# Pinning TensorE to "turn two groups, then multiply two groups" in a 30-step recurrence, with the first copy out of PSUM cut in two

## The chip, the cores and the metric

The kernel runs on one core of one Trainium2 chip. The metric is the device time of one execution in microseconds (us); lower is better. Engines are named as the profile names them: PE is TensorE's matmuls and PEld its weight loads, DVE is VectorE, ACT is ScalarE, POOL is GpSimd, and SP is the engine that issues most DMAs.

## The reference: what is computed

The input x has 3327 rows of 256 numbers. Two layers follow, each a graph attention and then a feed-forward part: in layer 0 a mixture of 16 experts, in layer 1 a recurrence over 30 steps. The change touches the recurrence alone. Cut to what matters, it is

```
def step(h, _):
    h = h + 0.01 * jnp.tanh(h)
    h = h * jax.nn.sigmoid(h)
    h = _layernorm(h, ln_w, ln_b)
    h = jnp.einsum('bsc,dc->bsd', h, W) + b
    return (h, None)
x, _ = jax.lax.scan(step, x, None, length=30)
```

Rows don't depend on each other. Each row goes through 30 steps in order, and its result is added to what came into the recurrence. Everything is fp32.

## The kernel before

The 3327 rows lie in SBUF as 26 tiles of 128 rows, `x` of 128 x 26 x 256. The recurrence works on groups of G = 4 tiles: six groups of four and a last one of two, seven in all (`groups`). Two nested loops, 30 steps outside and seven groups inside, emit this for each group (lines 992 to 1029):

- ScalarE makes `th = tanh(hs / S)` of the group (L998). The state is kept scaled by S = 100, so that POOL's sum `th + hs` (L1000) is the scaled `h + 0.01 tanh(h)`. ScalarE's Silu of it gives `z` (L1001).
- VectorE takes the statistics of each tile (`bn_stats`, L1006), and TensorE turns the tile by two 128 x 128 transposes into `pt` in PSUM (L1008): eight transposes for a group of four tiles. `pt` takes two PSUM banks, two tiles in each.
- `inv_norm` (L981 to L990) aggregates the statistics on VectorE (`v`, L986) and raises the variance to the power -1/2 on POOL (`rr`, L988 and L989).
- ScalarE copies the whole of `pt` to `zT` in SBUF, in one instruction (L1010).
- TensorE multiplies: for each tile two matmuls over the halves of the 256 features into `po` in PSUM (L1014). The weight that is loaded is a 128 x 128 piece of `zT`, and the matrix `wc` streams past it. An fp32 matmul stands in the profile as two records and a transpose as one; so a group of four has 8 transposes and 16 product records.
- VectorE scales by `rr` and adds the bias `bb`, tile by tile, back into `x` (L1019). The mean of the layer norm was folded into `wc` before.
- In the last step alone, a DMA brings what came into the recurrence (`old`, L1025), VectorE adds it (L1026) and DMAs write the output (L76).

The order of the work is not written by hand. The program is traced in Python, and a scheduler of the framework then orders each engine's instructions by its own estimates of time, taking the one traced first where several are ready. That order is fixed in the program: on the chip each engine works through its own list and waits on semaphores. Buffers limit how far it can run ahead: `th`, `z`, `zT`, `pt` and `po` have two buffers each, the small tiles of statistics four. In the step shown further down, TensorE's list has the runs that the timeline shows: 16 transposes, 32 product records, and at the end of a step runs of 10, 8 and 10.

Other stages matter only for comparison. In the projection of layer 1, `turned` (L141 to L149) turns two tiles by four transposes (L147), ScalarE copies one bank (L148), and `products` (L158 to L165) multiplies the two tiles turned before them (L162).

The lines about the copy and the two loops:

```
                for j in range(n):
                    nc.vector.bn_stats(stats[:, j, :], z[:, j, :])
                    for k in range(KD):
                        nc.tensor.transpose(pt[:, j, k, :], z[:, j, k * P : (k + 1) * P], ident)
                rr = inv_norm(stats, n)
                nc.scalar.copy(zT[:, :n, :, :], pt[:, :n, :, :])
```

Of the kernel before, what the change touches and what calls it, by code (L numbers as in the profile page):

```python
# [11 lines left out]
F32 = mybir.dt.float32  # L12
# [3 lines left out]
AF = mybir.ActivationFunctionType  # L16
ALU = mybir.AluOpType
# [3 lines left out]
P = 128  # L21
ALPHA = 0.2
EPS = 1e-5
N_STEPS = 30
S = 100.0
G = 4
# [4 lines left out]
def gat_moe_gat_recurrent_ffn(ctx: ExitStack, tc: tile.TileContext, a: dict, out: bass.AP):  # L31
    nc = tc.nc
    N, D = a["x"].shape
    KD = D // P
# [9 lines left out]
    groups = [range(t, min(t + G, NT)) for t in range(0, NT, G)]  # L44
# [9 lines left out]
    def spread(n):  # L54

        cut = n - n % 16
        return [r for r in ((0, cut), (cut, n)) if r[0] < r[1]]
# [6 lines left out]
    small = ctx.enter_context(tc.tile_pool(name="small", bufs=4))  # L64
# [3 lines left out]
    x = state.tile([P, NT, D], F32, name="x")  # L68
# [4 lines left out]
    def move_pairs(dram, tile, c0, c1, into_dram):  # L73

        def move(dst, src):
            nc.sync.dma_start(*((dst, src) if into_dram else (src, dst)))  # L76

        full = min(c1, PAIRS - 1)
        if full > c0:
            move(  # L80
                dram[c0 * 2 * P : full * 2 * P, :].rearrange("(t p b) d -> p t (b d)", p=P, b=2),
                tile[:, : 2 * (full - c0), :].rearrange("p (t b) d -> p t (b d)", b=2),
            )
        if c1 == PAIRS:
            base, last = (PAIRS - 1) * 2 * P, 2 * (PAIRS - 1 - c0)
            for r0, r1 in spread(REST // 2):
                move(
                    dram[base + 2 * r0 : base + 2 * r1, :].rearrange("(p b) d -> p (b d)", b=2),
                    tile[r0:r1, last : last + 2, :].rearrange("p b d -> p (b d)"),
                )  # L90
            if REST % 2:
                move(dram[base + REST - 1 : base + REST, :], tile[REST // 2 : REST // 2 + 1, last, :])
# [265 lines left out]
    with ExitStack() as moe:  # L358
# [5 lines left out]
        part = route_p.tile([P, 1], F32, name="part")  # L364
# [16 lines left out]
        ps_o = moe.enter_context(tc.tile_pool(name="ps0o", bufs=2, space=PSUM))  # L381
# [5 lines left out]
        with ExitStack() as pre:  # L387
# [83 lines left out]
            for k in range(2):  # L471
                numbers(pair[:, :, k, 0], [[P, NT]], k * NP, 1)
            nc.gpsimd.affine_select(
                out=before, in_=ones, pattern=[[1, P]], compare_op=ALU.is_gt, fill=0.0, base=0, channel_multiplier=-1
# [144 lines left out]
        two = rec.tile([P, 2, SLOTS], F32, name="prod")  # L619
# [252 lines left out]
        bb = rec.tile([P, D], F32, name="bb")  # L872
# [17 lines left out]
    kept = dram.tile([NP, D], F32, name="kept")  # L890
    steps = ctx.enter_context(tc.tile_pool(name="steps", bufs=2))
    with ExitStack() as st:
# [8 lines left out]
        ps_o = st.enter_context(tc.tile_pool(name="ps2o", bufs=2, space=PSUM))  # L901
# [74 lines left out]
    with ExitStack() as st:  # L976
        ps_t = st.enter_context(tc.tile_pool(name="ps3t", bufs=2, space=PSUM))
        ps_o = st.enter_context(tc.tile_pool(name="ps3o", bufs=2, space=PSUM))
        last_p = st.enter_context(tc.tile_pool(name="last", bufs=2))

        def inv_norm(stats, n):  # L981


            v = small.tile([P, G, 2], F32, name="v")
            for j in range(n):
                nc.vector.bn_aggr(v[:, j, :], stats[:, j, :])  # L986
            r = small.tile([P, G], F32, name="rr")
            nc.gpsimd.tensor_scalar(r[:, :n], v[:, :n, 1], EPS, None, op0=ALU.add)  # L988
            nc.gpsimd.tensor_tensor(r[:, :n], r[:, :n], neg_half[:, :n], ALU.pow)  # L989
            return r  # L990

        for step in range(N_STEPS):
            for ts in groups:
                n = len(ts)
                hs = x[:, ts[0] : ts[0] + n, :]
                th = steps.tile([P, G, D], F32, name="th")
                z = steps.tile([P, G, D], F32, name="z")
                nc.scalar.activation(th[:, :n, :], hs, AF.Tanh, scale=1.0 / S)  # L998

                nc.gpsimd.tensor_tensor(th[:, :n, :], th[:, :n, :], hs, ALU.add)  # L1000
                nc.scalar.activation(z[:, :n, :], th[:, :n, :], AF.Silu, scale=1.0 / S)  # L1001
                stats = small.tile([P, G, 6], F32, name="stats")
                pt = ps_t.tile([P, G, KD, P], F32, name="pt")
                zT = steps.tile([P, G, KD, P], F32, name="zT")
                for j in range(n):
                    nc.vector.bn_stats(stats[:, j, :], z[:, j, :])  # L1006
                    for k in range(KD):
                        nc.tensor.transpose(pt[:, j, k, :], z[:, j, k * P : (k + 1) * P], ident)  # L1008
                rr = inv_norm(stats, n)
                nc.scalar.copy(zT[:, :n, :, :], pt[:, :n, :, :])  # L1010
                po = ps_o.tile([P, G, D], F32, name="po")
                for j in range(n):
                    for k in range(KD):
                        nc.tensor.matmul(  # L1014
                            po[:, j, :], lhsT=zT[:, j, k, :], rhs=wc[:, k, :],
                            start=(k == 0), stop=(k == KD - 1),
                        )
                for j in range(n):
                    nc.vector.scalar_tensor_tensor(  # L1019
                        x[:, ts[0] + j, :], po[:, j, :], rr[:, j : j + 1], bb, op0=ALU.mult, op1=ALU.add  # L1020
                    )
                if step == N_STEPS - 1:
                    here = slice(ts[0] * P, (ts[-1] + 1) * P)
                    old = last_p.tile([P, G, D], F32, name="old")
                    nc.sync.dma_start(old[:, :n, :], kept[here, :].rearrange("(t p) d -> p t d", p=P))  # L1025
                    nc.vector.scalar_tensor_tensor(  # L1026
                        hs, hs, 1.0 / S, old[:, :n, :], op0=ALU.mult, op1=ALU.add
                    )
                    move_pairs(out, hs, ts[0] // 2, (ts[-1] + 1) // 2, True)


# [47 lines left out]
```

The softmax here doesn't subtract the row's maximum and nothing guards it: scores larger than these inputs give would overflow.

## Time and profile before

| what | us |
|---|---|
| three runs, without the profiler | 1998.33, 2000.29, 2000.75; median 2000.29 |
| the profiled execution, its own time | 2004.62 |
| its span, first to last instruction | 2002.9 |
| first transpose of the recurrence to the end of the span | 1098.5 to 2002.9 |
| ten steps of the recurrence, 1400 to 1699: PE, DVE, ACT, POOL busy | 291.95, 218.46, 188.99, 236.43 of 299 |
| TensorE's granted clock in that stretch | 1.00 of full speed |

The profile is of one execution. In a timeline each line is a run of equal instructions on one engine: its start in us from the start of the span, its length, the engine, the line of the kernel, output and inputs, shapes, count, and in brackets how long the engine had idled before and which engine's instruction ended that. In the list of groups, a line has the count, then the busy time in us and the mean length of one in ns, then the idle time ahead of them and its enders. Records of matmuls overlap each other, since their ends are modelled; the time between two starts is the measure of their rate.

### The profile page before, as it was taken

The page shows a single profiled execution, that of the slowest core. Times are in us where ns is not written, and L with a number is a line of the kernel's source. Part 1 is how long each engine was busy: PE and PEld are TensorE (multiplying, and loading weights), DVE is VectorE, ACT ScalarE, POOL GpSimd, SP SyncE. Part 2 cuts the span into 40 slices and gives each one's busy share as a digit, 9 for nine tenths or more (in the row PEclk, how much of TensorE's full clock was granted, in tenths as well). Part 3 has the DMA queues.
Part 4 walks back from the last instruction along what each step waited for, and adds up shares of the span by engine and source line. Part 5 has one row for each costly group of instructions (what it writes and reads, how often), then busy time and mean ns, then how long its engine had stood idle before and what let it go on. Part 6 is the DMA issues. An engine that isn't in the chain of part 4 may idle for free.

```text
span 2002.9 us, 33524 instructions
## 1 busy us (share of the span) xinstructions
PE 1930.9 (96%) x12032; PEld 1750.0 (87%) x12032; DVE 1299.7 (65%) x3827; ACT 1095.5 (55%) x1419; POOL 938.4 (47%) x864
## 2 busy tenths in 40 slices
PE   7999999999999997999999999999999999999998
PEld 6999999989999986888888888888888888888887
DVE  6887888722222226567576777777777777777777
ACT  2967766621111115566555666666666666666664
POOL 3020212443333321001000787787787787787785
PEclk9999999999999998999999999999999999999999
DMA  8978141189999854000001000000000000000003
GB/s 165 119 100 119 10 76 50 39 291 324 351 330 308 297 195 137 9 8 17 9 17 35 1 1 1 1 1 1 1 1 1 1 1 1 1 1 1 1 1 116
DMA packets 139754, 157.08 MB, mean 78 GB/s; under 512 B 52027, under 2 KB 99364, under 8 KB 139586
## 3 DMA queue, kind: packets, MB, share of 16 engines
q1 hardware_dynamic: 123466, 122.05, 19.8%
q0 software_dynamic: 11440, 28.09, 8.1%
q10 hardware_dynamic: 4680, 4.76, 0.7%
q8 instruction: 98, 1.61, 0.3%
q14 instruction: 70, 0.57, 0.1%
HBM read 164.58 MB, written 29.78 MB: 97 GB/s over the span
## 4 chain that ended last, share of the span: by engine, by line
PE 68%; issue 9%; ACT 5%; POOL 5%; DVE 4%; DMA 3%; SPq 0%; another core or an unknown queue 0%; POOLq 0%; DVEq 0%; ACTq 0%
PE po L1014 35%; PE acc L262 23%; PE pt L1008 5%; ACT zT L1010 5%; DVE pT L257 2%; POOL given L831 2%; POOL rb L730 2%; DMA given<-wh,to 2%; PE bank L786 2%; PE acc L827 1%; PE bank L499 1%; PE bank L221 0%; DVE x L913 0%; PE acc L162 0%; POOL rstd L120 0%
## 5 line engine op out<-in xcount | busy, mean ns | idle before, releaser
L1014 PE MATMUL po<-wc,zT 128*128 128x256 f32 x3120 | 705.5, 383 | 21.7 <-ACT zT L1010 21.1
L1014 PEld LDWEIGHTS po<-wc,zT 128*128 128x128 f32 x3120 | 583.1, 190 | 124.1 <-ACT zT L1010 49.7
L252 ACT ACTIVATE e<-rb,minus,full 128x384 f32<-128x384 f32 (+3 forms) x494 | 400.2, 824 | 180.9 <-DVE pT L257 162.7
L1000 POOL TENSOR_TENSOR th<-th,x 128x1024 f32<-128x1024 f32 (+1 forms) x210 | 460.8, 2213 | 64.3 <-ACT th L998 62.7
L257 DVE SCALAR_TENSOR_TENSOR pT<-e,part,adjT 128x384 f32<-128x384 f32 (+3 forms) x494 | 381.1, 776 | 138.1 <-PE acc L262 117.5
L1019 DVE SCALAR_TENSOR_TENSOR x<-po,rr,bb 128x256 f32<-128x256 f32 x780 | 324.9, 478 | 118.3 <-PE po L1014 113.8
L1010 ACT COPY zT<-pt 128x1024 f32<-128x1024 f32 (+1 forms) x210 | 199.0, 947 | 334.0 <-PE pt L1008 334.0
L1006 DVE BATCH_NORM_STATS2 stats<-z 128x6 f32<-128x256 f32 x780 | 283.7, 415 | 117.6 <-ACT z L1001 117.6
L262 PE MATMUL acc<-wh,pT 128*128 128x129 f32 x2704 | 310.4, 276 | 1.8 <-DVE pT L257 1.8
L262 PEld LDWEIGHTS acc<-wh,pT 128*128 128x128 f32 x2704 | 305.2, 192 | 2.5 <-DVE pT L257 2.4
L262 PE MATMUL acc<-s_wh,pT 128*128 128x257 f32 x1352 | 295.3, 380 | 0.8 <-DVE pT L257 0.7
L262 PEld LDWEIGHTS acc<-s_wh,pT 128*128 128x128 f32 x1352 | 255.9, 190 | 37.7 <-DVE pT L257 1.8
L120 POOL TENSOR_TENSOR rstd<-ve,neg_half 128x4 f32<-128x4 f32 (+3 forms) x28 | 30.4, 1086 | 415.7 <-DVE ve L118 332.1
L989 POOL TENSOR_TENSOR rr<-rr,neg_half 128x4 f32<-128x4 f32 (+1 forms) x210 | 208.0, 990 | 17.4
L1001 ACT ACTIVATE z<-th 128x1024 f32<-128x1024 f32 (+1 forms) x210 | 210.6, 1003 | 0.6 <-POOL th L1000 0.5
L998 ACT ACTIVATE th<-x 128x1024 f32<-128x1024 f32 (+1 forms) x210 | 199.3, 995 | 1.9 <-DVE x L127 0.9
L1008 PE MATMUL pt<-ident,z 128*128 128x128 f32 x1560 | 191.6, 274 | 2.5 <-DVE high L944 2.5
L1008 PEld LDWEIGHTS pt<-ident,z 128*128 128x128 f32 x1560 | 179.5, 142 | 14.9 <-issue 2.9
L786 PEld LDWEIGHTS bank<-hT,wh 128*128 128x128 f32 x1280 | 150.7, 194 | 9.2 <-issue 4.8
L786 PE MATMUL bank<-hT,wh 128*128 128x128 f32 x1280 | 151.8, 277 | 6.6 <-issue 2.2
L820 DVE TENSOR_TENSOR pT<-e,bank 128x512 f32<-128x512 f32 x61 | 41.9, 687 | 176.9 <-PE bank L786 124.2
L816 ACT ACTIVATE e<-bank 128x512 f32<-128x512 f32 x61 | 36.4, 597 | 194.1 <-PE bank L786 90.3
(189 smaller groups left out, 1346.4 us busy)
## 6 DMA issues: line engine op xcount, KB each, us to landing
wh<-in_w_dram SPq DMA_DIRECT2D x120, 512.0 KB
first_set<-in_w_dram SPq DMA_DIRECT2D x63, 512.0 KB
in_bytes<-in_adj_dram POOLq DMA_DIRECT2D x3, 2496.0 KB
x<-in_x_dram SPq DMA_DIRECT2D x6, 512.0 KB
kept<-x SPq DMA_DIRECT2D x8, 384.0 KB
old<-kept SPq DMA_DIRECT2D x6, 512.0 KB
out_dram<-x SPq DMA_DIRECT2D x6, 512.0 KB
table_x<-row ACTq DMA_DIRECT2D x3, 768.0 KB
```

The source lines that it names most:

```text
L252: nc.scalar.activation(e[:, : n * P], rb[:, : n * P], AF.Relu, scale=sc.full[:, j, h : h + 1], bias=sc.minus[:, j, h : h + 1],)
L257: masked = nc.vector.scalar_tensor_tensor(pT[:, : n * P], e[:, : n * P], sc.part[:, j, h : h + 1], adjT[:, j // 2, ts[0] * P : (ts[-1] + 1 ...
L262: nc.tensor.matmul(po[c], lhsT=pT[:, c * P : (c + 1) * P], rhs=wh[:, j, h, :], start=(j == 0 and c % per_bank == 0), stop=(j == NT - 1), s ...
L786: nc.tensor.matmul(p[:, f, :], lhsT=w[:, k, f * P : (f + 1) * P], rhs=hT[:, k, :], start=(k == 0), stop=(k == KD - 1),)
L989: nc.gpsimd.tensor_tensor(r[:, :n], r[:, :n], neg_half[:, :n], ALU.pow)
L1000: nc.gpsimd.tensor_tensor(th[:, :n, :], th[:, :n, :], hs, ALU.add)
L1001: nc.scalar.activation(z[:, :n, :], th[:, :n, :], AF.Silu, scale=1.0 / S)
L1006: nc.vector.bn_stats(stats[:, j, :], z[:, j, :])
L1008: nc.tensor.transpose(pt[:, j, k, :], z[:, j, k * P : (k + 1) * P], ident)
L1010: nc.scalar.copy(zT[:, :n, :, :], pt[:, :n, :, :])
L1014: nc.tensor.matmul(po[:, j, :], lhsT=zT[:, j, k, :], rhs=wc[:, k, :], start=(k == 0), stop=(k == KD - 1),)
L1019: nc.vector.scalar_tensor_tensor(x[:, ts[0] + j, :], po[:, j, :], rr[:, j : j + 1], bb, op0=ALU.mult, op1=ALU.add)
```

## The change

The body of the loop is cut into two functions. `turn_group` holds everything up to the transposes. `next_state` holds the rest: the power, the copy, the products and the update. The 210 parts (30 steps of seven groups, in one sequence across the ends of steps) are taken two at a time: two turns, then two next states. Each transpose and each matmul of the recurrence is passed to `tc.keep_in_program_order`, a method of the framework that puts an instruction behind the one traced just before it on the same engine; it orders the list and adds no wait. So TensorE's list is the traced order: turn A, turn B, products of A, products of B, then the next two. The other engines' lists are still the scheduler's. The copy of the first group of each two is made in pieces of two tiles (`pieces` = 2: two instructions for a group of four tiles, one for the group of two); the second group's copy stays whole.

```diff
-        for step in range(N_STEPS):
-            for ts in groups:
...
+        def turn_group(ts):
...
+            pt = ps_t.tile([P, G, KD, P], F32, name="pt")
+            for j in range(n):
+                nc.vector.bn_stats(stats[:, j, :], z[:, j, :])
+                for k in range(KD):
+                    tc.keep_in_program_order(
                         nc.tensor.transpose(pt[:, j, k, :], z[:, j, k * P : (k + 1) * P], ident)
-                rr = inv_norm(stats, n)
-                nc.scalar.copy(zT[:, :n, :, :], pt[:, :n, :, :])
-                po = ps_o.tile([P, G, D], F32, name="po")
-                for j in range(n):
-                    for k in range(KD):
+                    )
+            return pt, stats
+
+        def next_state(step, ts, pt, stats, pieces):
+            n = len(ts)
+            hs = x[:, ts[0] : ts[0] + n, :]
+            rr = inv_norm(stats, n)
+            zT = steps.tile([P, G, KD, P], F32, name="zT")
+            for c in range(0, n, G // pieces):
+                some = slice(c, min(c + G // pieces, n))
+                nc.scalar.copy(zT[:, some, :, :], pt[:, some, :, :])
+            po = ps_o.tile([P, G, D], F32, name="po")
+            for j in range(n):
+                for k in range(KD):
+                    tc.keep_in_program_order(
                         nc.tensor.matmul(
                             po[:, j, :], lhsT=zT[:, j, k, :], rhs=wc[:, k, :],
                             start=(k == 0), stop=(k == KD - 1),
                         )
...
+        parts = [(step, ts) for step in range(N_STEPS) for ts in groups]
+        for i in range(0, len(parts), 2):
+            two = [part + turn_group(part[1]) for part in parts[i : i + 2]]
+            for part, pieces in zip(two, (2, 1)):
+                next_state(*part, pieces)
```

More of the change, by code (lines that the diff above doesn't have):

```diff
@@ L990, in inv_norm @@
             return r
-        for step in range(N_STEPS):
-            for ts in groups:
[L994 to L1004, printed above, removed]
-                for j in range(n):
-                    nc.vector.bn_stats(stats[:, j, :], z[:, j, :])
-                    for k in range(KD):
-                        nc.tensor.transpose(pt[:, j, k, :], z[:, j, k * P : (k + 1) * P], ident)
-                rr = inv_norm(stats, n)
-                nc.scalar.copy(zT[:, :n, :, :], pt[:, :n, :, :])
-                po = ps_o.tile([P, G, D], F32, name="po")
-                for j in range(n):
-                    for k in range(KD):
@@ new lines, in turn_group @@
+        def turn_group(ts):
+            n = len(ts)
+            hs = x[:, ts[0] : ts[0] + n, :]
+            th = steps.tile([P, G, D], F32, name="th")
+            z = steps.tile([P, G, D], F32, name="z")
+            nc.scalar.activation(th[:, :n, :], hs, AF.Tanh, scale=1.0 / S)
+            nc.gpsimd.tensor_tensor(th[:, :n, :], th[:, :n, :], hs, ALU.add)
+            nc.scalar.activation(z[:, :n, :], th[:, :n, :], AF.Silu, scale=1.0 / S)
+            stats = small.tile([P, G, 6], F32, name="stats")
+            pt = ps_t.tile([P, G, KD, P], F32, name="pt")
[3 more added lines that the diff above has]
+                    tc.keep_in_program_order(
+                        nc.tensor.transpose(pt[:, j, k, :], z[:, j, k * P : (k + 1) * P], ident)
+                    )
+            return pt, stats
@@ new lines, in next_state @@
+        def next_state(step, ts, pt, stats, pieces):
+            n = len(ts)
+            hs = x[:, ts[0] : ts[0] + n, :]
+            rr = inv_norm(stats, n)
[7 more added lines that the diff above has]
+                    tc.keep_in_program_order(
@@ L1017, in gat_moe_gat_recurrent_ffn @@
                         )
-                for j in range(n):
-                    nc.vector.scalar_tensor_tensor(
-                        x[:, ts[0] + j, :], po[:, j, :], rr[:, j : j + 1], bb, op0=ALU.mult, op1=ALU.add
-                    )
[L1022 to L1029, printed above, removed]
+                    )
+            for j in range(n):
+                nc.vector.scalar_tensor_tensor(
+                    x[:, ts[0] + j, :], po[:, j, :], rr[:, j : j + 1], bb, op0=ALU.mult, op1=ALU.add
+                )
+            if step == N_STEPS - 1:
+                here = slice(ts[0] * P, (ts[-1] + 1) * P)
+                old = last_p.tile([P, G, D], F32, name="old")
+                nc.sync.dma_start(old[:, :n, :], kept[here, :].rearrange("(t p) d -> p t d", p=P))
+                nc.vector.scalar_tensor_tensor(hs, hs, 1.0 / S, old[:, :n, :], op0=ALU.mult, op1=ALU.add)
+                move_pairs(out, hs, ts[0] // 2, (ts[-1] + 1) // 2, True)
+        parts = [(step, ts) for step in range(N_STEPS) for ts in groups]
[3 more added lines that the diff above has]
+                next_state(*part, pieces)
 _OUT = ((3327, 256), "float32")
```

## The prediction

> **What bounds the kernel now.** I read four views in this order. First the page: TensorE's busy share, and the costliest groups.
>
> ```profile
> PE 1930.9 (96%) x12032; PEld 1750.0 (87%) x12032; DVE 1299.7 (65%) x3827; ACT 1095.5 (55%) x1419; POOL 938.4 (47%) x864
> ...
> L1014 PE MATMUL po<-wc,zT 128*128 128x256 f32 x3120 | 705.5, 383 | 21.7 <-ACT zT L1010 21.1
> L1014 PEld LDWEIGHTS po<-wc,zT 128*128 128x128 f32 x3120 | 583.1, 190 | 124.1 <-ACT zT L1010 49.7
> L1010 ACT COPY zT<-pt 128x1024 f32<-128x1024 f32 (+1 forms) x210 | 199.0, 947 | 334.0 <-PE pt L1008 334.0
> ```
>
> See that TensorE and ScalarE wait for each other over one edge, the copy zT. Records of matmuls overlap (383 ns each, started 216 ns apart), so "busy" and the 21.7 us of idle time hide what a wait costs. Second, therefore, TensorE's timeline, read by start times: one step of the recurrence, 1426.15 back to 1396.25, lasts 29.90 us.
>
> ```profile
> 1407.85 1.91 PE L1008 MATMUL pt<-ident,z 128*128 128x128 f32 x16
> 1409.99 7.17 PE L1014 MATMUL po<-wc,zT 128*128 128x256 f32 x32 [0.23 <-ACT zT L1010]
> 1417.00 1.91 PE L1008 MATMUL pt<-ident,z 128*128 128x128 f32 x16
> 1419.14 7.17 PE L1014 MATMUL po<-wc,zT 128*128 128x256 f32 x32 [0.23 <-ACT zT L1010]
> 1426.15 1.26 PE L1008 MATMUL pt<-ident,z 128*128 128x128 f32 x10
> 1427.43 1.99 PE L1014 MATMUL po<-wc,zT 128*128 128x256 f32 x8
> 1429.26 1.25 PE L1008 MATMUL pt<-ident,z 128*128 128x128 f32 x10
> 1430.74 7.17 PE L1014 MATMUL po<-wc,zT 128*128 128x256 f32 x32 [0.23 <-ACT zT L1010]
> ```
>
> TensorE already turns two groups and then forms two products in most places. The rate inside a run: transposes (1.91 - 0.273)/15 = 0.109 us; product records, from the second (1410.31) to the thirty-first (1416.57) of one run, 6.26/29 = 0.216 us. A pair at these rates is 16 x 0.109 + 32 x 0.2157 = 8.65 us; it takes 1417.00 - 1407.85 = 9.15. So **0.50 us is lost per pair**: 0.39 ahead of the first product (2.14 against 1.74) and 0.11 behind it (7.01 against 6.90). At the end of a step (10, 8, 10) the 8-record run loses 0.19 + 0.10 = 0.29. A step loses 3 x 0.50 + 0.29 = 1.79; check: 26 tiles need 52 x 0.109 + 104 x 0.2157 = 28.1, and 29.9 are spent.
>
> Third, ScalarE beside it, and VectorE:
>
> ```profile
> 1408.93 1.01 ACT L1010 COPY zT<-pt 128x1024 f32<-128x1024 f32 x1 [3.43 <-PE pt L1008]
> 1409.84 1.06 ACT L1001 ACTIVATE z<-th 128x1024 f32<-128x1024 f32 x1
> ```
>
> ```profile
> 1408.12 1.66 DVE L1019 SCALAR_TENSOR_TENSOR x<-po,rr,bb 128x256 f32<-128x256 f32 x4 [1.18 <-PE po L1014]
> ```
>
> ScalarE had idled 3.43 us when the first group was turned. Its eighth transpose starts at 1407.85 + 7 x 0.109 = 1408.62; the copy starts 0.31 later, takes 1.01, and the product's weight load starts 0.05 after it: 1.37 us from the eighth transpose, while the second group's eight transposes cover only 0.87. The VectorE line matters below: the second group's four tiles wait for the last of its products (a run of 32 that began at 1400.84), though the first two tiles, one PSUM bank, were done some 1.7 us earlier.
>
> Fourth, what an unhindered switch costs, from the layer-1 projection (TensorE, its loads, ScalarE):
>
> ```profile
> 764.04 0.67 PE L147 MATMUL bank<-ident,x 128*128 128x128 f32 x4
> 764.55 0.60 PE L162 MATMUL acc<-wv,hT 128*128 128x258 f32 x2
> 764.98 0.60 PE L147 MATMUL bank<-ident,x 128*128 128x128 f32 x4
> 765.42 2.41 PE L162 MATMUL acc<-wv,hT 128*128 128x258 f32 x10
> ```
>
> ```profile
> 765.38 2.04 PEld L162 LDWEIGHTS acc<-wv,hT 128*128 128x128 f32 x10
> ```
>
> ```profile
> 764.75 0.59 ACT L148 COPY hT<-bank 128x512 f32<-128x512 f32 x1 [1.07 <-PE bank L147]
> ```
>
> At 765.42 the product starts 0.11 after the last transpose (764.98 + 3 x 0.109 = 765.31), as inside a run. The load started 0.07 after that transpose, just behind a half-size copy of 0.59 us (764.75 + 0.59 + 0.04); the cost appears in the next record, 0.29 instead of 0.22 later: 0.07 us.
>
> **What the skill says.** "Trainium Kernel Development and Optimization", Performance Expectations, calls matmul busy time a bad metric; the trace agrees (97% busy with 0.50 of 9.15 us lost). "TensorE: Matmul & The Clock Gate", Step-by-step, says that a weight load is pulled ahead of matmuls in flight; here loads start about 0.1 us before their matmul, and this is what a wait exposes. "ScalarE: Activation LUTs", What ACT_TABLE_LOAD costs, gives 186 ns + 0.833 ns per element and 93 ns of overlap: 613 and 1039 ns for 512 and 1024 elements; the trace's 587 and 1010 are used. "PSUM — Partial Sum Buffer", PSUM bank collisions, says to guard PSUM by bank. The first piece is exactly one bank (two tiles of 1 KB), so it could start after four transposes; the VectorE line above shows this program guarding a two-bank tile as a whole instead.
>
> **The change, part by part.** *The order.* Counts of transposes and products stay. Groups 0 to 6 are odd in number, so two steps make seven pairs: five of 4+4 tiles, one of 2+4, one of 4+2. Pinned order alone brings little: a 4+4 pair costs what it costs now, 0.50.
>
> *The two pieces.* Counting from a pair's first transpose, with the guard over the whole tile: the eighth transpose starts at 0.76; piece one runs 1.07 to 1.66; its load can start at 1.71. In a 4+4 pair the last of 16 transposes starts at 1.64, so the load is 0.07 late, as at 765.38: cost **0.07** instead of 0.50. In 2+4 (one copy of two tiles, 0.64 to 1.22, load 1.27, last transpose 1.20) also 0.07. In 4+2 the last of 12 transposes starts at 1.20, the load is 0.51 late: cost 0.51 - 0.11 + 0.11 = 0.51. Two steps lose 6 x 0.07 + 0.51 = 0.94 instead of 3.58. Piece two runs 1.57 to 2.15; the ninth record, the first that reads it, loads at about 3.5: free.
>
> *Sum.* Now 30 x 1.79 = 53.7; minus 0.5 for the first pair (its products start at 1101.87, 0.2 after the last transpose) and 0.3 for the last group, behind which VectorE's work and the output DMA (1997.47 to 2002.9) set the end: 52.9. After: 15 x 0.94 = 14.1. Saved 38.8, less 0.2 because the tail behind group 5's products, which holds VectorE's work for both last groups, no longer starts before the last small turn: **38.6 us**.
>
> *What lies beside it, at nothing.* ScalarE gets 2 x 0.59 - 0.09 instead of 1.01 per pair, 0.1 more; its 3.4 us of idle time per pair hides that (uncovered, it would be 105 x 0.1 = 11 us). What is queued behind: Silu for the next pair starts 0.1 later and is needed a pair later. VectorE (21.8 of 29.9 us a step) and POOL (23.6) must fit in 28.6: 76% and 83%. POOL's cycle is two adds 4.69, two powers with their sums 2.7, 7.4 in all of 8.7 us. Tanh of a group follows its last update by about a pair, so the recurrence itself doesn't bind. Pinned TensorE can wait for a Silu result that it formerly stepped around; z is made half a pair to a pair ahead, so I take 0, bound 0 to 0.4 us for each of the 15 cross-step pairs (6 us). No DMA moves: the loads of "old" and stores on SP's queue keep their place behind each group's update.
>
> The profiled execution (2004.62, span 2002.9) would become 1966.0, its span 1964.3. The runs' median lies 4.3 below the profiled one; the same saving gives 2000.3 - 38.6 = **1961.7**.
>
> **Rivals.** (A) *Guard by bank.* Piece one starts after four transposes: 0.33 + 0.31 = 0.64, load at 1.27. A 4+4 pair loses nothing, 4+2 and 2+4 0.07 each: 15 x 0.14 = 2.1 instead of 14.1, time **1949.7**. For it: the size of the piece; against: VectorE's wait for all four tiles. (B) *POOL becomes the bound.* Its cycle now is 4.69 + 1.35 + 1.83 waiting + 1.35 = 9.2, the old pair. If the 1.83 (for VectorE's v) stays, nothing is won, **2000**; half of it gives 1981. Against: that wait hangs on Silu behind the copies, which moves with the turn. (C) *The pieces don't act apart*: the first product waits for both. Load at 2.20: 4+4 loses 0.56, 4+2 1.00, 2+4 0.07: 15 x 3.87 = 58, 5 more than the 52.9 of now, **2006**. Against: VectorE's per-tile statistics in one SBUF tile are waited for one by one. (D) *Slower by ScalarE's fixed order*: a Silu (1.06) of the next pair, which becomes ready when turning frees its buffer, is placed ahead of piece one. The load comes 0.97 later: 105 pairs x 0.97 = 102 on top of 14, against 52.9: **2064**. It decides from (52.9 - 14.1)/105 = 0.37 us of delay per pair. Against: now the copy goes first, in the same contest.
>
> **How the numbers follow.** Chances: forecast 0.62 (1957 to 1968, the upper end with the 6 us above), A 0.20 (1947 to 1953), B and lesser gains 0.10, C 0.02, D 0.06. Forecast and A hold 0.82: range 1947 to 1968. Bounds: 0.2%, 4 us, is about what a measurement of this kernel can tell from no change. Faster: 0.62 + 0.20 + 0.08 of B = 0.90; same 0.02 of B; slower 0.08 (C and D).
>
> **What would show it.** Right: runs of 16 and 32 throughout, 12 and 24 at step ends; product's idle time near 0 save once in two steps; a pair at 8.7 us; two copies of 587 ns, the first 0.31 after the eighth transpose. A: 0.31 after the fourth. Wrong: TensorE's transposes waiting for z, an ACTIVATE between turn and first copy, or POOL without idle time.

## The result, and the profile after

The changed kernel takes 1964.96 us (median of four runs, 1964.0 to 1967.98) against 1999.31 for the kernel before in runs beside it: ratio 0.982, 95% interval 0.9808 to 0.9833, so 33 to 38 us are saved (34 between the medians) where 38.6 were forecast. 1965.0 lies in the forecast's own range (1957 to 1968).

The page after, the same groups (lines 1014 and 1010 of before are 1024 and 1019 now):

```profile
PE 1908.9 (97%) x12032; PEld 1747.3 (89%) x12032; DVE 1281.6 (65%) x3827; ACT 1096.5 (56%) x1509; POOL 936.5 (48%) x864
...
L1024 PE MATMUL po<-wc,zT 128*128 128x256 f32 x3120 | 700.3, 382 | 3.6 <-ACT zT L1019 3.6
L1024 PEld LDWEIGHTS po<-wc,zT 128*128 128x128 f32 x3120 | 583.0, 190 | 89.0 <-ACT zT L1019 11.2
...
L1019 ACT COPY zT<-pt 128x512 f32<-128x512 f32 (+1 forms) x300 | 196.7, 721 | 294.1 <-PE pt L1008 294.1
```

Of the products' idle time, 21.7 us, 3.6 are left, and loads wait 11.2 us for the copy instead of 49.7. The busy share rose by one point only. Here are two stretches of TensorE's timeline, a 4+4 pair with a 2+4 pair, and the 4+2 pair some us later:

```profile
1457.19 1.91 PE L1008 MATMUL pt<-ident,z 128*128 128x128 f32 x16
1458.94 7.14 PE L1024 MATMUL po<-wc,zT 128*128 128x256 f32 x32
1465.92 1.47 PE L1008 MATMUL pt<-ident,z 128*128 128x128 f32 x12
1467.23 5.54 PE L1024 MATMUL po<-wc,zT 128*128 128x256 f32 x24
1472.61 1.91 PE L1008 MATMUL pt<-ident,z 128*128 128x128 f32 x16
```

```profile
1490.05 1.47 PE L1008 MATMUL pt<-ident,z 128*128 128x128 f32 x12
1491.77 5.45 PE L1024 MATMUL po<-wc,zT 128*128 128x256 f32 x24 [0.24 <-ACT zT L1019]
1497.05 1.91 PE L1008 MATMUL pt<-ident,z 128*128 128x128 f32 x16
```

Read by starts: the 4+4 pair takes 1465.92 - 1457.19 = 8.73 us, where it took 9.15, and the wait ahead of its products is gone (1.75 from transposes to products). The 2+4 pair takes 6.69 and the 4+2 pair 7.00; at the rates inside a run both would take 12 x 0.1092 + 24 x 0.2157 = 6.49. ScalarE beside them, at the 2+4 pair of 1465.92 and, in the last line, at a 4+4 pair that begins at 1481.33:

```profile
1466.55 0.59 ACT L1019 COPY zT<-pt 128x512 f32<-128x512 f32 x1 [2.94 <-PE pt L1008]
1467.03 1.06 ACT L1001 ACTIVATE z<-th 128x1024 f32<-128x1024 f32 x1
1467.99 1.00 ACT L1019 COPY zT<-pt 128x1024 f32<-128x1024 f32 x1
...
1482.40 1.99 ACT L1019 COPY zT<-pt 128x512 f32<-128x512 f32 x3 [3.37 <-PE pt L1008]
```

At 1482.40 three copies stand in one run. The first starts 1.07 us after the first transpose of its pair: 0.76 for eight transposes, and 0.31. So it waits for all eight, not for the four of its bank. VectorE still takes the second group's four tiles together, as before:

```profile
1466.19 1.66 DVE L1030 SCALAR_TENSOR_TENSOR x<-po,rr,bb 128x256 f32<-128x256 f32 x4 [1.18 <-PE po L1024]
```

**The account.** For every pair I took the time from its first transpose to the next run of transposes, less 0.1092 us per transpose and 0.2157 per product record, the rates inside a run. Summed over the recurrence this loss of TensorE's falls from 54.6 to 17.3 us, by 37.3. (The last pair, which no transposes follow, isn't in the sum.) The 17.3 are 74 pairs of 4+4 with 0.07, 14 of 4+2 with 0.51, 15 of 2+4 with 0.21, and the first pair of all with 1.67.

That first pair has nothing to do with the copy: it loses 1.70 before, too. TensorE's granted clock is 0.83 of full speed over the first 10 us of the recurrence in both traces, and the transposes of this pair start 0.213 us apart instead of 0.109. All traces show such a loss but that of e3 below, where the clock is 1.00; why isn't known. The first line is of before, the second of e3:

```profile
1098.51 3.57 PE L1008 MATMUL pt<-ident,z 128*128 128x128 f32 x16 [2.49 <-DVE high L944]
1091.66 1.94 PE L1008 MATMUL pt<-ident,z 128*128 128x128 f32 x16 [2.49 <-DVE high L944]
```

Without the first pair the loss is 52.9 us before and 15.7 after. From the first transpose to the end of the span it is 904.4 us before and 868.3 after: 36.1 saved. The profiled spans differ by more, 40.3 us, because the recurrence began 4.2 us earlier in the trace of after, behind stages that the change doesn't touch; experiments below began up to 6.9 us earlier than before. For single traces, therefore, I compare from the first transpose on.

### The profile page after: what moved, and what is told of

The parts are those of the page before. It is cut to its first block, busy times and chain, and to the rows that moved or that the text cites. A ratio compares the mean times of both kernels' runs of the same rounds, so it can differ in the third digit from the quotient of the medians.

```text
span 1962.6 us, 33704 instructions
## 1 busy us (share of the span) xinstructions
PE 1908.9 (97%) x12032; PEld 1747.3 (89%) x12032; DVE 1281.6 (65%) x3827; ACT 1096.5 (56%) x1509; POOL 936.5 (48%) x864
## 4 chain that ended last, share of the span: by engine, by line
PE 71%; issue 9%; POOL 5%; DVE 4%; DMA 3%; ACT 1%; SPq 0%; POOLq 0%; DVEq 0%; ACTq 0%
PE po L1024 35%; PE acc L262 24%; PE pt L1008 8%; POOL given L831 2%; DVE pT L257 2%; POOL rb L730 2%; DMA given<-wh,to 2%; PE bank L786 1%; PE bank L499 1%; DMA wh<-in_w_dram 1%; DMA lists<-pair,ati 1%; DVE x L913 1%; PE bank L221 0%; PE acc L162 0%; ACT zT L1019 0%
## 5 line engine op out<-in xcount | busy, mean ns | idle before, releaser
L1024 PEld LDWEIGHTS po<-wc,zT 128*128 128x128 f32 x3120 | 583.0, 190 | 89.0 <-ACT zT L1019 11.2
L1005 DVE BATCH_NORM_STATS2 stats<-z 128x6 f32<-128x256 f32 x780 | 275.1, 413 | 168.5 <-ACT z L1001 168.5
L1019 ACT COPY zT<-pt 128x512 f32<-128x512 f32 (+1 forms) x300 | 196.7, 721 | 294.1 <-PE pt L1008 294.1
L262 PEld LDWEIGHTS acc<-s_wh,pT 128*128 128x128 f32 x1352 | 255.9, 190 | 37.7 <-DVE pT L257 1.8
L1001 ACT ACTIVATE z<-th 128x1024 f32<-128x1024 f32 (+1 forms) x210 | 201.6, 1011 | 0.6 <-POOL th L1000 0.5
```

Of the source, the lines that this page charges most:

```text
L262: nc.tensor.matmul(po[c], lhsT=pT[:, c * P : (c + 1) * P], rhs=wh[:, j, h, :], start=(j == 0 and c % per_bank == 0), stop=(j == NT - 1), s ...
L1024: nc.tensor.matmul(po[:, j, :], lhsT=zT[:, j, k, :], rhs=wc[:, k, :], start=(k == 0), stop=(k == KD - 1),)
```

## The experiments

In each, "loss" is the sum just described, the first pair included (1.5 to 1.8 us; in e3 0.03).

**What the pin itself does: nothing here.** Without `keep_in_program_order`, and with all else of the change, the scheduler gives all five engines the same lists with the same waits; so it does for the copies of e1, e3, e4 and e7. So there is no run without the pin: the new order comes from the traced order alone (two turns, then two next states). Where the prediction and the expectations say "pinned", read "traced in this order".

**e1: the new order alone.**

```diff
-            for part, pieces in zip(two, (2, 1)):
+            for part, pieces in zip(two, (1, 1)):
```

> The new order with every copy whole. Theory (the cut of the copy makes the gain; a product waits for its copy, and the order alone covers no more of it than before): a pair of 4+4 loses 0.50 us again, 4+2 0.94, 2+4 0.21, so 54.7 us in all against 54.6 before: about 2000, level with the kernel before. Rival (fixing the order makes the gain): about 1965.

Measured: 2002.42 us, ratio 1.001 (1.0003 to 1.0017); loss 54.6. TensorE's timeline of e1:

```profile
1507.35 1.47 PE L1008 MATMUL pt<-ident,z 128*128 128x128 f32 x12
1509.49 5.45 PE L1024 MATMUL po<-wc,zT 128*128 128x256 f32 x24 [0.67 <-ACT zT L1019]
1514.78 1.91 PE L1008 MATMUL pt<-ident,z 128*128 128x128 f32 x16
1516.91 7.17 PE L1024 MATMUL po<-wc,zT 128*128 128x256 f32 x32 [0.23 <-ACT zT L1019]
1523.92 1.91 PE L1008 MATMUL pt<-ident,z 128*128 128x128 f32 x16
```

The 4+4 pair takes 9.15 us again. Order alone gains nothing; the 4+2 pair even loses 0.94 (7.43 against 6.49), which with the 0.21 of a 2+4 pair balances the old ends of steps. With the same loss e1 is still some 2 us slower: behind its last product record 7.2 us pass to the end of the span, where it was 5.7 before. The rival falls.

**e2: the cut alone**, in the loop of the kernel before.

```diff
-                nc.scalar.copy(zT[:, :n, :, :], pt[:, :n, :, :])
+                for c in range(0, n, G // 2):
+                    nc.scalar.copy(zT[:, c : c + 2, :, :], pt[:, c : c + 2, :, :])
```

> The loop of the kernel before, group by group, with each copy cut in two and nothing pinned. TensorE's list then changes: six transposes of the next group stand between a group's last transpose and its products, instead of eight. Theory (what counts is when the first piece lands, against the transposes that cover it): piece one lands and its load starts 0.95 us after the eighth transpose, the cover is 0.65, so 0.29 lost per group, 7 x 0.29 = 2.1 us a step instead of 1.8: about 2006, slower than before by 7. Rival (the cut makes the gain whatever the order): about 1965.

Measured: 2006.88 us, ratio 1.0035 (1.0024 to 1.0047); loss 59.6. TensorE and ScalarE of e2:

```profile
1504.21 1.04 PE L1008 MATMUL pt<-ident,z 128*128 128x128 f32 x8
1505.27 3.72 PE L1015 MATMUL po<-wc,zT 128*128 128x256 f32 x16
1508.83 0.82 PE L1008 MATMUL pt<-ident,z 128*128 128x128 f32 x6
```

```profile
1504.63 1.07 ACT L1011 COPY zT<-pt 128x512 f32<-128x512 f32 x2 [1.49 <-PE pt L1008]
```

The list is now one turn, one product. Of the eight transposes at 1504.21 two finish a group and six begin the next. The copy starts 0.31 after the second of them (1504.32), ends 0.59 later, and the product at 1505.27 comes 1.06 after the run's first transpose instead of 0.87: 0.19, and 0.11 behind it. So the pieces alone make the kernel slower: in the new list six transposes cover each group's copy, where before the first group of a pair had eight, and the second had the first one's products. That the scheduler goes to the product earlier because its own estimate has the first piece ready earlier is likely, but not shown. Of these two, order and cut, neither gains anything alone; together they do.

**e3: one tile per bank.**

```diff
-            pt = ps_t.tile([P, G, KD, P], F32, name="pt")
+            pt = [ps_t.tile([P, G // 2, KD, P], F32, name=f"pt{q}") for q in range((n + 1) // 2)]
...
-                nc.scalar.copy(zT[:, some, :, :], pt[:, some, :, :])
+                nc.scalar.copy(zT[:, some, :, :], pt[c // 2][:, : min(2, n - c), :, :])
...
-            for part, pieces in zip(two, (2, 1)):
+            for part, pieces in zip(two, (2, 2)):
```

> As the changed kernel, with pt as two tiles of one bank each, and so both groups' copies in two pieces. Theory (the first piece waits for all eight transposes only because they write one tile): piece one starts 0.31 us after the fourth transpose; 4+4 loses nothing, 4+2 and 2+4 0.07 each; 17.3 us of loss become about 3: 1965 - 14 = 1951. Rival (the first piece is held by something else, or the remaining loss lies elsewhere): 1963 to 1965, as with both copies cut.

Measured: 1950.4 us, ratio 0.9752 (0.9739 to 0.9766), clear of the changed kernel's interval; loss 2.6. TensorE and ScalarE of e3:

```profile
1503.79 1.91 PE L1008 MATMUL pt<-ident,z 128*128 128x128 f32 x16
1505.54 7.07 PE L1024 MATMUL po<-wc,zT 128*128 128x256 f32 x32
1512.45 1.47 PE L1008 MATMUL pt<-ident,z 128*128 128x128 f32 x12
1513.76 5.41 PE L1024 MATMUL po<-wc,zT 128*128 128x256 f32 x24
1519.01 1.91 PE L1008 MATMUL pt<-ident,z 128*128 128x128 f32 x16
```

```profile
1504.43 2.05 ACT L1019 COPY zT<-pt 128x512 f32<-128x512 f32 x4 [3.24 <-PE pt L1008]
```

The copy starts 0.64 after the pair's first transpose: 0.33 for four, and 0.31. A 4+4 pair takes 8.66, its rate without a loss. What held the first piece was that both banks were one tile to the program, not PSUM itself. With e5 below, from which the runs can't tell it apart, this is the fastest version here.

**e4: both copies cut**, one tile: only `(2, 1)` becomes `(2, 2)`. It is also the control of e3.

> As the changed kernel, with the second group's copy in two pieces too. Theory (in a 2+4 pair the second copy, whole, lands too late: 0.21 lost where I had said 0.07): the 15 pairs of 2+4 lose 0.07, so 2 us less than the changed kernel: 1963; the other pairs stay at 0.07 and 0.51. Rival (the 0.21 comes from something else): 1965, and 2+4 pairs stay at 0.21.

Measured: 1961.67 us, ratio 0.9808 (0.9795 to 0.9822); loss 15.4. The interval overlaps that of the changed kernel, so the runs don't resolve the 2 us; the trace does. The 2+4 pair of e4:

```profile
1522.18 1.47 PE L1008 MATMUL pt<-ident,z 128*128 128x128 f32 x12
1523.49 5.41 PE L1024 MATMUL po<-wc,zT 128*128 128x256 f32 x24
1528.74 1.91 PE L1008 MATMUL pt<-ident,z 128*128 128x128 f32 x16
```

It takes 6.56 instead of 6.69 and loses 0.07; the other pairs lose 0.07 and 0.51 as in the changed kernel. So 0.13 of the 0.21 belonged to the second group's whole copy. TensorE's list is the same in e3 and e4 (in the other engines' lists some entries move); of the 12.8 us of loss between them, 1.7 are the clock in the first pair, and the other 11.1 come from splitting the tile. The medians differ by 11.3.

**e5 and e6: the cut elsewhere.** One tile for `pt`; the first copy is cut after one tile, or after three, the second in halves.

```diff
-            for c in range(0, n, G // pieces):
-                some = slice(c, min(c + G // pieces, n))
+            for c, e in zip(pieces, pieces[1:]):
+                some = slice(c, min(e, n))
+                if c >= n:
+                    break
...
-            for part, pieces in zip(two, (2, 1)):
+            for part, pieces in zip(two, ((0, 1, 4), (0, 2, 4))):
```

(e6 has (0, 3, 4) for (0, 1, 4).)

> One tile for pt, as in the changed kernel; the first group's copy is cut after one tile instead of two, the second's in halves. Theory (the loss is how much later the first piece's load comes than the last transpose, and nothing else): piece one of about 0.38 us starts 0.31 after the eighth transpose, its load 0.05 behind it at 1.50, before the last of 16 transposes (1.64): 4+4 loses nothing, 4+2 0.30, 2+4 nothing; 4.5 us of loss where both copies cut in halves lose 15.4: 1962 - 11 = 1951. Rival (only an earlier start than the eighth transpose can help): 1962.

> The same with the cut after three tiles. Theory: piece one takes about 0.80 us, its load comes at 1.92: 4+4 loses 0.28, 4+2 0.72, 2+4 0.07; 15 x (5 x 0.28 + 0.72 + 0.07) = 33 us of loss instead of 15.4: 1962 + 17 = 1979. Rival (any cut is as good): 1962.

Measured: e5 1952.92 us, ratio 0.9759 (0.9746 to 0.9773), loss 6.4. e6 1981.16 us, ratio 0.9904 (0.9889 to 0.9919), loss 34.1. A 4+4 pair of e5, with its copies, and one of e6:

```profile
1500.86 1.91 PE L1008 MATMUL pt<-ident,z 128*128 128x128 f32 x16
1502.61 7.07 PE L1026 MATMUL po<-wc,zT 128*128 128x256 f32 x32
1509.52 1.91 PE L1008 MATMUL pt<-ident,z 128*128 128x128 f32 x16
```

```profile
1501.93 2.05 ACT L1021 COPY zT<-pt 128x256 f32<-128x256 f32 x4 [2.81 <-PE pt L1008]
```

```profile
1503.00 1.91 PE L1008 MATMUL pt<-ident,z 128*128 128x128 f32 x16
1504.92 7.17 PE L1026 MATMUL po<-wc,zT 128*128 128x256 f32 x32
1511.93 1.91 PE L1008 MATMUL pt<-ident,z 128*128 128x128 f32 x16
```

e5's first copy still starts 1.07 after the pair's first transpose, yet the pair takes 8.66: a piece that is short enough needs no earlier start. e6's pair takes 8.93, and 0.29 is lost. The rivals of both fall.

**e7: the copy queued late**, for the price of rival D.

```diff
+            if pieces == 2:
+                junk = steps.tile([P, G, KD, P], F32, name="junk")
+                nc.scalar.copy(junk[:, :n, :, :], pt[:, :n, :, :])
             for c in range(0, n, G // pieces):
```

> The changed kernel with one more instruction on ScalarE: a whole copy of the first group's pt into an unused tile, traced ahead of the two pieces, so that it becomes ready with them and goes first. It stands for anything of 1 us that ScalarE's list places ahead of the copy (rival D). Theory: the first piece starts 0.92 later in pairs that begin with four tiles, 0.49 later in the other; 4+4 loses 0.99, 4+2 1.43, 2+4 0.57: 104 us of loss instead of 17: 1965 + 87 = 2052. Rival (ScalarE's 3 us of idle time per pair cover it): 1965 to 1970.

Measured: 2051.89 us, ratio 1.0261 (1.0246 to 1.0277); loss 103.2. TensorE and ScalarE of e7:

```profile
1509.26 1.91 PE L1008 MATMUL pt<-ident,z 128*128 128x128 f32 x16
1511.89 7.17 PE L1027 MATMUL po<-wc,zT 128*128 128x256 f32 x32 [0.72 <-ACT zT L1022]
1518.90 1.91 PE L1008 MATMUL pt<-ident,z 128*128 128x128 f32 x16
```

```profile
1510.33 1.01 ACT L1019 COPY junk<-pt 128x1024 f32<-128x1024 f32 x1 [1.70 <-PE pt L1008]
1511.24 2.00 ACT L1022 COPY zT<-pt 128x512 f32<-128x512 f32 x3
```

ScalarE idled 1.70 us just ahead of this copy, and that covers nothing: the copy still starts 1.07 after the pair's first transpose, 0.31 after the eighth. A pair takes 9.64. The rival falls.

Over the 4+4 pairs, the load's lateness after the start of the last transpose, as worked out beforehand, and the loss as measured are: -0.14 and 0.01 (e5), 0.07 and 0.07 (changed), 0.28 and 0.29 (e6), 0.50 and 0.50 (e1), 0.99 and 0.99 (e7).

## Why the prediction was right

- *The bound and the size of the wait.* The forecast put what the change could win at 52.9 us. The sum of before, 54.6, is 52.9 without the first pair, whose 1.70 neither kernel avoids. With the copies whole, e1 has all of it again (54.6).
- *Order alone brings little.* Right: e1, 1.001.
- *The guard over the whole tile*, the choice between the forecast and rival A. Right: the first piece starts 0.31 after the eighth transpose. It was read off VectorE's line, a consumer of another two-bank tile; e3 shows that it is the tile. Rival A's time, 1949.7, is close to what e3 measures (1950.4) once the tile is split, though e3 also cuts the second copy, which A left whole. The Trainium skill's advice to guard PSUM by bank ("PSUM — Partial Sum Buffer", PSUM bank collisions) is what e3 comes to: with a tile for each bank the copy starts 0.31 after the fourth transpose, the last into its bank. The two-bank tile is guarded more widely than that advice asks.
- *A pair of 4+4 loses 0.07, one of 4+2 0.51.* Right.
- *A pair of 2+4 loses 0.07.* This term was mis-sized: 0.21, so 15 x 0.13 = 2.0 us more. I had priced the second group's copy at nothing without looking at what covers it. In a 2+4 pair only eight product records do. The copy stands behind a Silu in ScalarE's list (1467.03) and ends at 1468.99, and the load of the ninth record starts at 1469.05. The eighth record starts at 1468.81, so the ninth is due at 1469.02. Counted from 0.11 before that (1468.92), its load is 0.13 late, and 0.13 is lost. e4 takes the term away.
- *The ends.* Up to the start of the last product record TensorE saves 37.7 us, where 38.8 were forecast: 2.0 fewer in the 2+4 pairs, and about 0.9 more in the last pair, which loses 1.00 before and 0.56 after, where I had 0 and 0.51. The tail from there to the end of the span is 7.2 us after and 5.7 before. It takes back 1.5, where I had allowed 0.2, and leaves the 36.1 of the trace. The products of the last two groups now come closer together than VectorE's updates: before, VectorE waited for the last of them (first line), and after, it comes to the last tile 2.0 us after the start of that tile's last record, without a wait (second line). The tail of e1 is as long, so it comes with the order.

```profile
1997.68 0.88 DVE L1019 SCALAR_TENSOR_TENSOR x<-po,rr,bb 128x256 f32<-128x256 f32 x2 [0.24 <-PE po L1014]
1957.35 0.48 DVE L1030 SCALAR_TENSOR_TENSOR x<-po,rr,bb 128x256 f32<-128x256 f32 x1
```

- *Rival B, POOL.* Wrong, as argued: its wait for VectorE's v shrinks when TensorE speeds up. The waits of before and of after, each over all but the ends of the recurrence:

```profile
POOL rr L988 <- DVE v L986: 114.8, 88, 3.3
...
POOL th L1000 <- ACT th L998: 56.9, 59, 5.5
```

```profile
POOL th L1000 <- ACT th L998: 112.1, 72, 6.3
...
POOL rr L988 <- DVE v L986: 30.4, 17, 4.1
```

  Part of it moves to the wait for Tanh, and TensorE doesn't see it: e3 comes within 2.6 us of TensorE's rates.
- *Rival C.* Wrong: in the pair that begins at 1481.33 the products start at 1483.08. The three copies end at 1484.39; the last of them is whole, takes 1.00 and overlaps the one ahead by about 0.09, so the second piece ends at about 1483.5, after the products have begun.
- *Rival D.* ScalarE's list kept the copy first, so it didn't occur. The way it was priced is right: in e7 the first piece starts 0.91 behind the added copy (1510.33 to 1511.24), and a 4+4 pair loses 0.91 more. The total, 102 on top of 14, is for a Silu that costs 0.97 in every pair, which no run has; e7's instruction costs less, and its loss is 103.2.

## What to carry to other kernels

Where an in-order engine waits for a copy of its own result, price the wait by one difference: when the first piece lands, against when the work that covers it ends; busy shares and idle sums hide most of it, so read starts. Cut the copy only together with the order of the work that covers it, for a scheduler that orders by its own estimates may spend the cut on a shorter cover. If consumers take a tile in parts, give each part a tile of its own, or else, as here, the first part waits for the whole; where that can't be done, make the first piece short enough to land under the cover (e5).

## What was not expected

From 0.07 to 0.99 us, lateness after the start of the last transpose turns into loss one to one. A load that waits for nothing starts with the matmul ahead of its own: 0.11 us before its own behind a transpose, and 0.22 behind a product record (1468.59, for the record at 1468.81), where the prediction had about 0.1 throughout. A load that comes 0.07 late leaves the distance from transpose to product at 0.11 and shows only in the second product record (0.29 instead of 0.22 after the first). So the idle time in brackets is 0.00 at a loss of 0.07 and 0.24 at a loss of 0.51.
